# Attention block on one core: the fifth visit's readers exchanged, dense matmuls put ahead of the value products, and the small steps between them rescheduled

## The chip, the core and the metric

The kernel runs on one core of one Trainium2 chip. A core has a matmul engine (PE, with PEld for its weight loads), a vector engine (DVE), an activation engine (ACT), a general engine (POOL) and a queue that issues transfers (SP), each with its own instruction stream[...]. The metric is the device time of one execution in microseconds (us).

## The reference

Input `x` is 4 batches of 512 tokens by 512 features. Everything is float32.

```
x = x + attention(layernorm(x))     # 32 query heads, 8 key/value heads, head size 16, rotary, causal
x = x + (silu(h @ Wg.T) * (h @ Wu.T)) @ Wd.T,   h = layernorm(x)      # inner size 1376
```

The softmax is over the keys of each query, with the query's own largest score taken off first.

## The kernel before

**Dense work.** Projections, the output projection and the feed-forward part are called dense work here. They are cut into steps of four matmuls, each matmul 32 output columns wide while attention runs (L240), so that four lie side by side in the array. Batch b's input is normalised, turned so that features lie on the partitions (`xnT`), and projected to queries, keys and values (`projections`, L327). Batches 0 and 2 are turned by PE (`transposed`, L242). Batches 1 and 3 are turned by DVE and transfers (`flipped`, L252): DVE transposes blocks into `xt`, SP writes them to `flip` in memory with four transfers (L259), and reads each tile of 128 tokens back into `xnT` with one (L261). The last tile's read has to wait for its own four writes.

**Groups.** Attention runs over 32 groups of four heads, eight groups a batch. The loop `slot(b, ...)` (L790) holds batch b's eight groups and fills the gaps between their score matmuls with dense steps of other work. While group g gets its final scores ("less", L557, whose query rows `qa` already hold the largest score), group g+2 gets plain scores (L544), of which DVE finds the largest for each query.

**Visits.** Each group has five visits to the two score tiles `sc`, of two PSUM banks each. In visits 1 to 4 the first tile always holds plain scores of two heads and the second holds less scores of the two other heads. DVE reads the first tile (`greatest`, L586), ACT takes the exponential of the second (L645), POOL zeroes what lies past the diagonal (`causal`, L647). The next visit's matmuls overwrite the same tiles. In visit 5 (`last_visit`, L607) every bank holds both kinds, less scores in its first half and plain ones in its second, so ACT and DVE both want each bank. ACT takes the first tile, then the second; DVE follows it, the first tile, then the second. The framework that records the kernel makes two readers of one bank wait for each other in program order. Then come the largest scores turned and written to memory (`turned_round`, L626), from where SP lays them into a later group's `qa` (`laid_out`, L633), and the value products `av` (`averages`, L664), which read the exponentials after POOL has zeroed them. POOL also makes a fresh `qa` (`masked`, L523, L529) right after visit 5's zeroing; the next visit 1 starts with it.

**Order of the work around the change.** `gap(n)` puts dense steps after visit n+1; in slot 0 (`thin`) the shares are 0.2, 0.225, 0.2875 and 0.2875 of a group's dense work, in the others five shares, the last after the value products. `odd_steps(us)` (L213) puts small steps of DVE behind each visit's `greatest`: first `later` if a value product is unread, then `aside` (statistics, normalisations, turning), then the filled projection banks of `full` (rotary: L303, L307 on DVE, L304, L308 on POOL), then the rest of `later`. `holding` makes `put` keep back some POOL instructions from the end of visit 4 until `release` after visit 5. Normalisation of batches 2 and 3 is a DVE shift (L198) and an ACT scaling (L199), not kept back. Batch 2's input is loaded in `begin2`, which the opening (L766 to L788), where groups 0 and 1 get their plain scores, calls among its dense steps.

Of the kernel before, what the change touches and what calls it, by code (L numbers as in the profile page):

```python
# [14 lines left out]
AF = mybir.ActivationFunctionType  # L15
# [3 lines left out]
B, T, D = 4, 512, 512  # L19
NH, NKV, DH = 32, 8, 16  # L20
FF = 1376
P = 128
NT = T // P
# [26 lines left out]
GROUPS = [(b, m, hf) for b in range(B) for m in range(4) for hf in range(2)]  # L50
# [24 lines left out]
def preln_block_kernel(  # L75
# [13 lines left out]
    nc = tc.nc  # L89
# [18 lines left out]
    for rows, at, base in ((slice(0, P), T - P, 0), (slice(0, 64), T, 64), (slice(64, P), T, 0)):  # L108
# [4 lines left out]
            fill=MASKED,  # L113
# [50 lines left out]
    full = deque()  # L164
# [14 lines left out]
    def load_xr(b, i):  # L179
        t = work.tile([P, D], F32, tag="xr", name="xr", bufs=6)  # L180
        nc.sync.dma_start(out=t, in_=x[b, ts(i, P), :])
        xr[b, i] = t

    def statistics(src):
        st = small.tile([P, 6], F32, tag="st", name="st")
        mv = small.tile([P, 2], F32, tag="mv", name="mv")
        rstd = small.tile([P, 1], F32, tag="rstd", name="rstd")
        nc.vector.bn_stats(st, src)  # L188
        nc.vector.bn_aggr(mv, st)
        nc.vector.tensor_scalar(rstd, mv[:, 1:2], EPS, None, ALU.add)  # L190
        nc.gpsimd.tensor_tensor(rstd, rstd, neghalf, ALU.pow)
        return src, mv, rstd

    def normalised(dst, found, by_act=False):
        src, mv, rstd = found
        if by_act:
            shift = mv[:, 1:2]
            nc.vector.tensor_scalar(shift, mv[:, 0:1], rstd, -1.0, ALU.mult, ALU.mult)  # L198
            nc.scalar.activation(dst, src, AF.Identity, bias=shift, scale=rstd)  # L199
        else:  # L200
            nc.vector.tensor_scalar(dst, src, mv[:, 0:1], rstd, ALU.subtract, ALU.mult)

# [7 lines left out]
        for _ in range(min(n, len(queue))):  # L210
            queue.popleft()[1]()

    def odd_steps(us, banks=True):  # L213

        for n in range(len(soon)):
            left, step = soon.popleft()
            if left > 0:
                soon.append((left - 1, step))
            else:
                aside.appendleft(step)  # L220
        while True:
            queue = (unread and later) or aside or (banks and full and full[0]) or later
            if not queue:
                return
            us -= queue[0][0]
            if us < -0.15:
                return
            do(queue)
            if full and not full[0]:
                full.popleft()  # L230
# [52 lines left out]
        steps = [lambda ps, k=k, h=h: product(ps, k, ts(h, 2 * P)) for h in range(2) for k in range(NK)]  # L283
        return [(0.43, step) for step in portions(steps, finish, 8)]

    held = deque()
    holding = [False]

    def put(step):
        held.append(step) if holding[0] else step()

    def release():
        while held:
            held.popleft()()

    def rotated(ps, dst, engine=nc.gpsimd):

        rot = work.tile([P, T], F32, tag="rot", name="rot", bufs=4)  # L300
# [23 lines left out]
            cost, step = steps[kind]  # L324
            yield cost, lambda step=step, i=int(i): step(i)

    def projections(b, n, early=False):  # L327

        home, xa, found, xn, ready = homes[n], {}, {}, {}, []
        xnT = xnT_of[b]  # L330

        def load(i):
            if early:
                xa[i] = xr[b, i]
            else:
                xa[i] = work.tile([P, D], F32, tag="xa", name="xa", bufs=4)
                nc.sync.dma_start(out=xa[i], in_=x[b, ts(i, P), :])

        def measure(i):
            found[i] = statistics(xa[i])  # L340

        def norm(i):
            xn[i] = work.tile([P, D], F32, tag="xa", name="xa", bufs=4) if early else xa[i]
            normalised(xn[i], found[i], by_act=b > 1)

        def flip(i):
            if b % 2:
                flipped(xn[i], i, 1, xnT)
            ready.append(i)

        def keys():
            def finish(ps):
                kr = work.tile([P, T], F32, tag="rot", name="kr", bufs=4)

                def spread():
                    release()
                    ks = work.tile([P, T], F32, tag="rot", name="ks", bufs=4)
                    nc.vector.stream_shuffle(ks, kr, SWAP)
                    for t, hf, src in ((0, 0, kr), (1, 1, kr), (0, 1, ks), (1, 0, ks)):
                        put(  # L360
                            lambda t=t, hf=hf, src=src: nc.gpsimd.tensor_scalar(
                                home[:, 4 + 2 * t + hf, :], src, halves[hf], (one16, one0)[hf], ALU.mult, ALU.add
                            )
                        )

                last = spread if early else lambda: soon.append((1, (0.75, spread)))
                return [*rotated(ps, kr, nc.vector if early else nc.gpsimd), (0.0, last)]

            return projected(wk_sb, 0, xnT, finish)

        def vals():
            def product(ps, i, k):
                for c in (0, 64) if i == NT - 1 else ():
                    token = P * i + 64 - c
                    product_of(
                        ps[c : c + 64, ts(i, P)], xnT[:, k, token : token + 64], wv_sb[:, k, :], k == 0, k == NK - 1
                    )
                if i < NT - 1:
                    product_of(ps[:, ts(i, P)], xnT[:, k, ts(i, P)], wv_sb[:, k, :], k == 0, k == NK - 1)

            def finish(ps):
                def copy():
                    nc.scalar.copy(
                        values(n)[:, :, :, DH : 2 * DH].rearrange("p i g d -> p (i g) d"),
                        ps.rearrange("p (a d) -> p a d", d=DH),
                    )

                return [(0.0, copy)]

            steps = [lambda ps, i=i, k=k: product(ps, i, k) for i in range(NT) for k in range(NK)]  # L390
            return [(0.45, step) for step in portions(steps, finish, 8)]

        def queries(m):
            engine = nc.vector if early and m == 0 else nc.gpsimd
            return projected(wq_sb, m, xnT, lambda ps: rotated(ps, home[:, m, :], engine))

        def begin():
            for i in range(NT):
                load(i)
            if b > 1:  # L400
                aside.extend(both_steps_apart(measure, norm, flip, 0.75 if b % 2 else 0.0))
            else:
                aside.extend(both_steps(measure, norm, flip, flip_us=0.75 if b % 2 else 0.0))

        def tail(i):
            while i not in ready:
                do(aside)
            if b % 2 == 0:
                transposed(xn[i], i, xnT)

        turned = [(0.0 if b % 2 else 0.45, lambda i=i: tail(i)) for i in range(NT)]
        rest = [*keys(), *queries(0), *vals()]
        for m in range(1, 4):
            rest += queries(m)
        return (0.0, begin), turned, rest

    def attended(b, by_pe=()):

# [188 lines left out]
    def last_visit(h, g):  # L607

        for r in range(4):
            less_score(g, r, 2, pairs[r // 2][:, r % 2, : 2 * P])  # L610
        if h < len(GROUPS):
            for half in (64, 0):
                for r in range(4):
                    plain_half(h, r, 1, pairs[r // 2][:, r % 2, 2 * P :], half)
        for n in (0, 1):
            heads = slice(2 * n, 2 * n + 2)
            exponentials(e2[:, heads, :], pairs[n][:, :, : 2 * P])
            causal(e2, 0, heads)
        holding[0] = False
        masked(g + 3)  # L620
        release()
        if h < len(GROUPS):
            for r in range(4):
                greatest(h, r, 1, pairs[r // 2][:, r % 2, 2 * P :])

    def turned_round(g):  # L626
        if g >= len(GROUPS):
# [90 lines left out]
    for t in low:  # L718
# [2 lines left out]
    nc.sync.dma_start(out=rope_sb, in_=rope)  # L721
    load_columns(wq_sb, wq, 0, P)

    (begin1, turned1, rest1), (begin2, turned2, rest2), (begin3, turned3, rest3) = (
        projections(b, b) for b in range(1, B)
    )
    begin, turned, start = projections(0, 0, early=True)
    begin[1]()
    do(aside, len(aside))
    begin1[1]()  # L730
# [34 lines left out]

    thin[0] = True  # L766
    opening = deque([*start[28:], *turned1, begin2, *rest1[:16]])
    each = sum(cost for cost, _ in opening) / 6
    done = 0.0
    for h in range(2):  # L770
        for n, entries in enumerate((((0, 3),), ((0, 2), (3 * P, 0)), ((0, 1),))):
# [8 lines left out]
            odd_steps((1.5, 1.0, 2.7 - h)[n])  # L780
            if h == 0:
                nc.gpsimd.memset(values(n + 1), 1.0)
            done = fill(opening, each * (3 * h + n + 1), done)
        if h == 0:
            laid_out(0)
            masked(2)
# [3 lines left out]
    def slot(b, steps):  # L790
# [7 lines left out]

        def gap(n):
            nonlocal done, part  # L800
            part += total * ((0.2, 0.225, 0.2875, 0.2875) if thin[0] else (0.19, 0.19, 0.22, 0.22, 0.18))[n] / 8
            done = fill(steps, part, done)

        for g in groups:
            h = g + 2
            laid_out(g + 1)
            for n, visit in enumerate(visits):
# [12 lines left out]
                    causal(e1, 3 * P, exchanged=True)  # L820
                all_greatest(h, visit)
                holding[0] = n == 3
                odd_steps((1.3, 0.95, 0.95, 1.05)[n] if thin[0] else 2.3, n < 3)
                gap(n)
            last_visit(h, g)
            turned_round(h)
            averages(g)
            odd_steps(1.4)
            if not thin[0]:
                gap(4)  # L830
        thin[0] = narrow[0] = False
        emptied(len(full))
        if b == B - 1:
# [90 lines left out]
```

## Time and profile before

| what | value |
|---|---|
| median of 3 runs (lowest to highest) | 893.87 us (893.75 to 894.65) |
| the profiled execution's own time | 893.94 us |
| its span | 892.2 us |
| PE busy | 865.6 us, 97% of the span |
| DVE busy | 469.6 us, 53% |
| POOL busy | 234.5 us, 26% |
| ACT busy | 204.6 us, 23% |
| slot 0, groups 0 to 7 | 51.38 to 179.03 us |
| slots 1 to 3 | 179.03 to about 734 us |
| dense tail on PE alone | to the end |

Times in the trace count from the first instruction. DVE is busy for 6 to 8 tenths of each fortieth of the span up to about 180 us and mostly for 4 to 5 tenths from there to the dense tail, and not at all evenly within a group: a share over the whole run says little about the place where a stage waits.

### The profile page before, as it was taken

Reading aid. Unit: us, or ns where it says so; the run is one execution under the profiler, and the core shown is the slowest. Engines: PE = TensorE matmul, PEld = TensorE weight load, DVE = VectorE, ACT = ScalarE, POOL = GpSimd, SP = SyncE. Lnnn points to the kernel's source line nnn. Section 1 sums busy time; section 2 is a strip of 40 time slices with the busy share of each in tenths; the row PEclk is TensorE's granted clock in tenths of the full one; section 3 lists DMA queues with packets and bytes.
Section 4 is the critical chain, followed back from the end, with each engine's and each line's share of the span. In section 5 each row is a group of like instructions: output and inputs, shape, how many; then the busy total and the mean of one; then the engine's idle time right before and its main releaser. Section 6 shows DMA issues by size and latency. Waiting matters only on the chain.

```text
span 892.2 us, 23910 instructions
## 1 busy us (share of the span) xinstructions
PE 865.6 (97%) x10142; PEld 352.8 (40%) x10142; DVE 469.6 (53%) x1481; ACT 204.6 (23%) x256; POOL 234.5 (26%) x358
## 2 busy tenths in 40 slices
PE   6989999998999999999999999999999999999998
PEld 5644444543333333333333333333333334444443
DVE  7886887777555554485554544575555214121110
ACT  1034443322232222222222222222222220000000
POOL 5555575653312112232112222231221211000000
PEclk9999999999999999999999999999999999999999
DMA  8410141005515110524121110242111203523000
GB/s 247 85 50 5 51 74 29 4 4 121 180 50 176 44 50 14 191 41 117 52 52 44 36 50 14 63 85 84 51 50 50 68 13 80 131 72 82 19 12 35
DMA packets 122762, 59.68 MB, mean 67 GB/s; under 512 B 60480, under 2 KB 114752, under 8 KB 122400
## 3 DMA queue, kind: packets, MB, share of 16 engines
q1 hardware_dynamic: 122368, 52.39, 22.6%
q10 hardware_dynamic: 288, 5.77, 1.7%
q8 instruction: 80, 1.31, 0.6%
q14 instruction: 26, 0.21, 0.1%
HBM read 44.76 MB, written 13.37 MB: 65 GB/s over the span
## 4 chain that ended last, share of the span: by engine, by line
PE 81%; DVE 10%; POOL 2%; DMA 2%; issue 2%; SPq 1%; ACT 1%; POOLq 0%; DVEq 0%; ACTq 0%
PE mm L240 41%; PE mm L237 17%; PE sc L544 12%; PE av L672 6%; DVE junk L590 5%; PE sc L557 4%; POOL e L650 1%; DVE st L188 1%; DVE rot L303 1%; ACT e L645 1%; POOL qa L529 1%; DMA lowest<-turned 1%; SPq L259 0%; PE mm L245 0%; DVE xr L440 0%
## 5 line engine op out<-in xcount | busy, mean ns | idle before, releaser
L590 DVE CUSTOM_DVE_ANT_0 junk<-sc,mask 128x128 f32<-128x128 f32 (+3 forms) x512 | 251.2, 491 | 155.9 <-PE sc L557 93.1
L240 PE MATMUL mm<-xnT,shared 128*32 128x512 f32 (+1 forms) x2704 | 281.9, 545 | 1.0 <-ACT xnT L250 1.0
L645 ACT ACTIVATE e<-sc 128x1024 f32<-128x1024 f32 (+1 forms) x192 | 165.5, 881 | 413.9 <-PE sc L557 334.8
L650 POOL TENSOR_SCALAR_AFFINE_SELECT e<-e 128x512 f32<-128x512 f32 (+2 forms) x192 | 105.6, 560 | 367.5 <-ACT e L645 364.4
L544 PE MATMUL sc<-home,qa 32*64 32x512 f32 (+6 forms) x2048 | 157.8, 422 | 10.9 <-DVE low L590 8.4
L557 PE MATMUL sc<-qa,home 32*64 32x512 f32 (+6 forms) x2048 | 153.1, 428 | 2.7 <-DVE low L590 2.2
L240 PEld LDWEIGHTS mm<-xnT,shared 128*32 128x32 f32 x2704 | 88.0, 109 | 157.5 <-issue 142.1
L544 PEld LDWEIGHTS sc<-home,qa 32*64 32x64 f32 x2048 | 67.4, 131 | 113.4 <-issue 39.6
L237 PE MATMUL mm<-xnT,shared 128*128 128x512 f32 (+2 forms) x256 | 94.7, 528 | 0.0
L240 PE MATMUL mm<-wd_sb,home 128*32 128x512 f32 (+1 forms) x808 | 94.7, 595 | 0.0
L672 PE MATMUL av<-e,home 128*32 128x512 f32 (+3 forms) x1024 | 80.6, 437 | 1.2 <-POOL e L650 1.1
L495 DVE SCALAR_TENSOR_TENSOR g<-g,mm 128x512 f32<-128x512 f32 (+1 forms) x44 | 30.3, 688 | 96.6 <-ACT g L494 96.6
L557 PEld LDWEIGHTS sc<-qa,home 32*64 32x64 f32 x2048 | 58.8, 130 | 31.8 <-issue 14.2
L237 PEld LDWEIGHTS mm<-xnT,shared 128*128 128x128 f32 (+1 forms) x256 | 48.0, 189 | 46.6 <-issue 44.7
L237 PE MATMUL mm<-wd_sb,home 128*128 128x512 f32 (+1 forms) x150 | 65.0, 593 | 0.0
L494 ACT ACTIVATE g<-mm 128x512 f32<-128x512 f32 (+1 forms) x44 | 26.3, 597 | 168.8 <-PE mm L237 109.6
L497 DVE TENSOR_TENSOR home<-mm,g 128x512 f32<-128x512 f32 (+1 forms) x44 | 30.4, 691 | 57.2 <-PE mm L240 34.0
L513 DVE SCALAR_TENSOR_TENSOR xr<-mm,xr 128x512 f32<-128x512 f32 x16 | 11.0, 689 | 76.4 <-PE mm L237 56.2
L672 PEld LDWEIGHTS av<-e,home 128*32 128x32 f32 x1024 | 31.1, 109 | 44.6 <-issue 36.6
L240 PEld LDWEIGHTS mm<-wd_sb,home 128*32 128x32 f32 (+1 forms) x808 | 28.3, 110 | 50.6 <-issue 49.6
L240 PE MATMUL mm<-wo_sb,cx 128*32 128x512 f32 x384 | 45.0, 595 | 0.0
L237 PEld LDWEIGHTS mm<-wd_sb,home 128*128 128x128 f32 (+1 forms) x150 | 28.4, 190 | 36.3 <-issue 36.3
(73 smaller groups left out, 454.0 us busy)
## 6 DMA issues: line engine op xcount, KB each, us to landing
shared<-in_wg SPq DMA_DIRECT2D x40, 256.0 KB
shared<-in_wu SPq DMA_DIRECT2D x40, 256.0 KB
flip<-xt SPq DMA_DIRECT2D x88, 64.0 KB
xnT<-flip SPq DMA_DIRECT2D x18, 256.0 KB
xr<-in_x SPq DMA_DIRECT2D x16, 256.0 KB
out<-xr SPq DMA_DIRECT2D x16, 256.0 KB
xa<-in_x SPq DMA_DIRECT2D x12, 256.0 KB
spill<-wd_sb ACTq DMA_DIRECT2D x1, 2816.0 KB
```

Source lines behind the costliest of these rows:

```text
L237: nc.tensor.matmul(out, lhsT=lhsT, rhs=rhs, start=start, stop=stop)
L240: nc.tensor.matmul(out[c : c + 32], lhsT=lhsT[:, c : c + 32], rhs=rhs, start=start, stop=stop)
L494: nc.scalar.activation(gs[f][:m, :], ps[:m, :], AF.Tanh, scale=0.5)
L495: nc.vector.scalar_tensor_tensor(gs[f][:m, :], gs[f][:m, :], 1.0, ps[:m, :], ALU.add, ALU.mult)
L497: nc.vector.tensor_tensor(homes[n][:m, f, :], ps[:m, :], gs[f][:m, :], ALU.mult)
L513: nc.vector.scalar_tensor_tensor(xr[b, i], py[i], 0.5, xr[b, i], ALU.mult, ALU.add)
L544: nc.tensor.matmul(dst[at : at + 64, :n], lhsT=qa[g][rows_of(r), q : q + 64], rhs=keys_of(g)[rows_of(r), :n], start=True, stop=True,)
L557: nc.tensor.matmul(dst[at : at + 64, first_q:], lhsT=keys_of(g)[rows_of(r), k : k + 64], rhs=qa[g][rows_of(r), P * j + first_q :], start=True,
L590: nc.vector.tensor_tensor_reduce(out=junk[:, :n], in0=src, in1=mask[:, T - n : T] if i else mask[:, T:], scale=-1.0, scalar=BIG, op0=ALU.a ...
L645: nc.scalar.activation(dst, src, AF.Exp, scale=1.0 / math.sqrt(DH))
L650: nc.gpsimd.affine_select(out=e[rows, heads, c : c + P], in_=e[rows, heads, c : c + P], compare_op=ALU.is_ge, fill=0.0, base=base, pattern ...
L672: nc.tensor.matmul(av[32 * r : 32 * r + 32, P * j :], lhsT=v[:, j, 4 * (m // 2) + r, DH * (1 - hf) : DH * (3 - hf)], rhs=e[:, r, c : c + n ...
```

## The change

Six edits, all in the order in which instructions are recorded; no arithmetic is added or removed.

1. In visit 5, DVE reads the second tile first while ACT takes the first, then they exchange. ACT's exponential of the second tile now waits for DVE's two reads there.
2. Dense steps stand between visit 5 and the value products in every slot. In slots 1 to 3 the fifth share moves there from behind the value products. In slot 0 a fifth share, 0.077, is new, and visits 2 to 4 give it up.
3. `odd_steps` may put rotary steps of a filled bank ahead of `aside` after visit 1.
4. ACT's scaling of batches 2 and 3 goes through `put`, so it is kept back from visit 4 to the end of visit 5 when its step falls there; `flip` releases it.
5. Batch 2's input is loaded when batch 1's last tile has been turned, not in `begin2`.
6. The opening's dense steps are spread 0.3, 0.38 and 0.32 over its three visits instead of evenly.

Edits 3 and 5 also shift small steps to other visits. On DVE in slot 0 the order behind each visit becomes the following (the groups of the loop; st = statistics, sh = shift, xt = turning, us = reading of `av`, cx = turning of the context, ks = key shuffle, rot and cos = rotary):

```
group: before visit 1's reads | after visit 1 | after 2 | after 3 | after 4     (before -> after)
0: st sh | st sh rot cos | st | ks sh rot cos | sh      ->  st sh | rot cos | st | ks sh rot cos | st
1: us | - | rot | cos | -                               ->  us sh sh | - | rot | cos | -
3: us | st sh | st rot cos | xt sh | st rot cos         ->  us | rot cos | st | st | sh rot cos
4: us | ks | xt sh | sh xt rot cos | xt                 ->  us | rot cos | ks | st | xt sh
5: cx | us | rot | cos | -                              ->  cx | us | st | xt sh | sh xt rot cos
6: us | rot cos | rot | cos | cx                        ->  us | rot cos | xt | rot | cx cos
```

On ACT the two scalings of batch 2's last tiles now stand together, behind group 0's fifth visit and ahead of the values' copy (L383) and of group 1's first exponential. On SP batch 2's four loads stand ahead of the first write of `lowest`. Batch 3's last tile is turned in group 6 (after visit 2) instead of group 4 (after visit 4). On PE the second half of batch 3's keys, which reads that tile's part of `xnT`, is in group 6 between visits 3 and 4.

```diff
@@ statistics / normalised
-            nc.scalar.activation(dst, src, AF.Identity, bias=shift, scale=rstd)
+            put(lambda: nc.scalar.activation(dst, src, AF.Identity, bias=shift, scale=rstd))
@@ odd_steps
-    def odd_steps(us, banks=True):
+    def odd_steps(us, banks=1):
...
-            queue = (unread and later) or aside or (banks and full and full[0]) or later
+            bank = full and full[0]
+            queue = (unread and later) or (banks == 2 and bank) or aside or (banks and bank) or later
@@ projections
-    def projections(b, n, early=False):
+    def projections(b, n, early=False, then=None):
...
         def flip(i):
+            if b > 1:
+                release()
             if b % 2:
                 flipped(xn[i], i, 1, xnT)
             ready.append(i)
+            if i == NT - 1 and then:
+                then()
...
-        def begin():
+        def load_all():
             for i in range(NT):
                 load(i)
+
+        def begin():
+            if not xa:
+                load_all()
@@ last_visit
         for n in (0, 1):
             heads = slice(2 * n, 2 * n + 2)
             exponentials(e2[:, heads, :], pairs[n][:, :, : 2 * P])
             causal(e2, 0, heads)
+            if h < len(GROUPS):
+                for r in (2 - 2 * n, 3 - 2 * n):
+                    greatest(h, r, 1, pairs[r // 2][:, r % 2, 2 * P :])
         holding[0] = False
         masked(g + 3)
         release()
-        if h < len(GROUPS):
-            for r in range(4):
-                greatest(h, r, 1, pairs[r // 2][:, r % 2, 2 * P :])
@@ the opening
-    (begin1, turned1, rest1), (begin2, turned2, rest2), (begin3, turned3, rest3) = (
-        projections(b, b) for b in range(1, B)
-    )
-    begin, turned, start = projections(0, 0, early=True)
+    begin3, turned3, rest3, _ = projections(3, 3)
+    begin2, turned2, rest2, load2 = projections(2, 2)
+    begin1, turned1, rest1, _ = projections(1, 1, then=load2)
+    begin, turned, start, _ = projections(0, 0, early=True)
...
-    each = sum(cost for cost, _ in opening) / 6
+    each = sum(cost for cost, _ in opening) / 2
...
-            done = fill(opening, each * (3 * h + n + 1), done)
+            done = fill(opening, each * (h + (0.3, 0.68, 1.0)[n]), done)
@@ slot
-            part += total * ((0.2, 0.225, 0.2875, 0.2875) if thin[0] else (0.19, 0.19, 0.22, 0.22, 0.18))[n] / 8
+            part += total * ((0.2, 0.2, 0.2615, 0.2615, 0.077) if thin[0] else (0.19, 0.19, 0.22, 0.22, 0.18))[n] / 8
...
-                odd_steps((1.3, 0.95, 0.95, 1.05)[n] if thin[0] else 2.3, n < 3)
+                odd_steps((1.3, 0.95, 0.95, 1.05)[n] if thin[0] else 2.3, (2, 1, 1, 0)[n])
                 gap(n)
             last_visit(h, g)
             turned_round(h)
+            gap(4)
             averages(g)
             odd_steps(1.4)
-            if not thin[0]:
-                gap(4)
```

## The prediction, made before the run

> **What bounds the kernel now.** I read the page's busy shares and its chain first, then the timeline of single groups, then windows at the places where groups differ.
>
> ```profile
> PE 865.6 (97%) x10142; PEld 352.8 (40%) x10142; DVE 469.6 (53%) x1481; ACT 204.6 (23%) x256; POOL 234.5 (26%) x358
> ...
> PE 81%; DVE 10%; POOL 2%; DMA 2%; issue 2%; SPq 1%; ACT 1%; POOLq 0%; DVEq 0%; ACTq 0%
> ```
>
> PE sets the end, and DVE is the only other engine with weight on the chain. Group starts (first plain scores in the timeline) tell where. In slots 1 to 3 most groups take 23.29 us or less, and PE has no wait but its own changes between dense and score matmuls. In slot 0 the starts are 51.38, 70.83, 86.01, 101.11, 117.49, 133.70, 148.78, 163.92 and 179.03, so groups last 19.45, 15.18, 15.10, 16.38, 16.21, 15.08, 15.14 and 15.11 us. There DVE paces PE: the interval between visits 3 and 4 is 3.0 us both with 12 dense matmuls (group 2) and with 16 (group 5), and the dense phase with its wait is 2.06 us in each. Moving dense work out of these visits saves nothing. Groups 0, 3 and 4 are longer because DVE's small steps overfill the cover that a visit's scores give them (0.95 to 1.05 us, about 1.15 to 1.25 with latency).
>
> An ordinary end of a group in slot 0, from the timeline:
>
> ```profile
> 160.49 0.69 PE L557 MATMUL sc<-qa,home 32*64 32x256 f32 x16
> 161.43 2.44 PE L672 MATMUL av<-e,home 128*32 128x512 f32 x32
> 161.63 1.08 ACT L645 ACTIVATE e<-sc 128x512 f32<-128x512 f32 x2 [1.89 <-PE sc L544]
> 162.26 0.42 DVE L590 CUSTOM_DVE_ANT_0 junk<-sc,mask 128x256 f32<-128x256 f32 x1 [1.20 <-ACT e L645]
> 162.35 0.83 POOL L650 TENSOR_SCALAR_AFFINE_SELECT e<-e 128x256 f32<-128x256 f32 x2 [0.62 <-ACT e L645]
> 163.17 0.69 POOL L529 TENSOR_SCALAR qa<-home,rope_sb 128x512 f32<-128x512 f32 x1
> 163.92 0.64 PE L544 MATMUL sc<-home,qa 32*64 32x512 f32 x2
> ```
>
> DVE waits 0.63 us for ACT's first exponential. The next visit 1 starts right after `qa` (163.86) and then pauses 0.33 us more for DVE's last bank.
>
> Where slot 0 starts, DVE waited for batch 2's input, PE stood still (49.56 to 51.38), and its clock was then granted at half:
>
> ```profile
> 48.11 0.69 DVE L188 BATCH_NORM_STATS2 st<-xa 128x6 f32<-128x512 f32 x1 [2.05 <-DMA xa<-in_x]
> ```
> ```profile
> 50.00:52.00 2.00, 0.62 (x4) 0.22 (x4) 1.79 (x8) 0.00 (x0) 1.92 (x2) 1.00 0.02 7
> 52.00:54.00 2.00, 2.00 (x15) 0.32 (x12) 1.52 (x7) 0.34 (x1) 0.96 (x2) 0.60 0.05 8
> 54.00:56.00 2.00, 2.00 (x42) 1.62 (x40) 1.59 (x5) 1.46 (x2) 0.14 (x1) 0.55 0.04 9
> ```
>
> (The last three numbers are granted clock, DMA share, GB/s.) Visit 1's scores took 2.89 us there instead of 1.04.
>
> **The opening and group 0.** The loads ahead of `lowest` end the 2.05 us wait. PE then comes to visit 1 at 49.5, when its dense work ends; DVE clears the second tile at 52.28 - 2.05 = 50.2; scores end near 51.15 instead of 54.27, at full clock. On SP the four loads cost 1.87 us of issue and 3.6 us of data (DMA share 0.96 at 47 to 48) ahead of `lowest` and the five `qa` transfers: group 0's rows land near 48.3 instead of 46.5 and are used at 49.5, so 0, and up to 1.0 if the queue is slower. From there POOL sets group 0's end: key shuffle (8 us after the scores), two L361 (1.52), rotary (1.28 + 1.27), visit 4's zeroing (1.92), the newly placed rstd (0.55), visit 5's zeroing (0.84), `qa` (0.69): 67.2 against 70.83. **-3.6**; bounds -2.4 (loads late, clock falls anyway) and -4.
>
> **Ordinary groups of slot 0.** DVE is ready 0.65 us earlier, so visit 1's pause of 0.33 goes. But ACT's second exponential now follows DVE's two reads (161.6 + 0.95), then come its 0.55, zeroing 0.41, `qa` 0.69: 164.25, 0.4 later than before; the new dense step (0.43) and `av` (2.4) end at the same time. **+0.05** a group, four or five of them: +0.2. This chain now has no slack, and a small step behind visit 4 over 1.1 us passes through whole (before, ACT's 0.6 covered it too).
>
> **Groups 1, 3, 4, 5.** Group 1: the two shifts wait for `us`, which waits for `av`. From the end of `av`: us and reciprocal 0.92, shifts 0.4, scalings from 1.14 to 2.76 (814 ns each), values' copy to 3.35 (585), exponential to 4.37 (1.02). Visit 2's less scores need that tile at about 2.9: +1.45, **+1.4** with visit 1's pause gone. Queued behind the wait on ACT: that copy and all exponentials. Group 3: 1.42 us behind visit 4 overfill by 0.3, and the double load behind visit 2 is gone: 16.38 to 15.45. Group 4: no overfill, 16.21 to 15.15. Together **-2.0**. Group 5: shift, turning and rotary (2.03) behind visit 4: **+0.9**.
>
> **Group 6.** Batch 3's last tile is turned behind visit 2's reads, and keys that read it come one dense step after visit 3's scores. The trace has every link:
>
> ```profile
> 33.03 0.71 DVE L255 STREAM_TRANSPOSE xt<-xa 128x512 f32<-128x512 f32 x1
> ...
> 33.76 1.93 SPq L259 DMA_DIRECT2D flip<-xt  x4
> 35.81 1.81 SPq L261 DMA_DIRECT2D wd_sb<-flip  x2
> ```
> ```profile
> 129.80 2.77 DMA xnT<-flip
> ```
>
> The last write is issued 1.45 after the transposition, the last tile's read at 37.24, 2.05 after that, and a read takes 2.7: 6.2 us. From group 6's start: visit 2's scores end at 3.7, DVE's reads at 5.15, transposition 5.8, data at 12.0. PE comes to these keys at 6.7 (visit 3 from 5.33, scores 0.95, one step 0.43). After the data two steps and the change (1.02) bring visit 4 at 13.0 instead of 8.34: +4.7, and nothing later hides it; behind it queue visit 4's scores, so DVE and ACT too. Before, the same read was issued at 134.59 and first used after 150. For the clock after this 5.3 us stand there are two answers. Here it fell after 1.82 us of stillness. The Trainium skill ("TensorE: Matmul & The Clock Gate", Part 1) lets it fall after an idle window of some 3.4 us that runs free, and rise after a busy one; by that page 5.3 us need not hold a whole window, and the price is between 0 and 1.7. By the row it falls surely: 3.4 us at half are 1.7, less what DVE's pace hides, 1.5. I take the row: **+6.2**; with the page's other end +4.7. The page would also have let the start of slot 0 keep its clock; the row of 52 to 54 says otherwise.
>
> **Slots 1 to 3.** The same dense work stands on the other side of `av`. Three waits lose their place: in group 8 `av` waited 0.7 for zeroing behind an rstd, and visit 1 0.33; group 9's visit 1 to 2 lost 0.9 to DVE's additions, whose matmuls now end 2.4 us earlier; group 16's `av` waited 0.7. Sum -2.7. The change from `av` to scores took 0.24 in slot 0, from dense 0.21: +0.03 for 22 groups, +0.6. **-2.1**; bounds -3.3 and -0.8. The longer wait of ACT's second exponential lies under 1.7 us or more of dense work and costs nothing; without that cover it is 0.4 a group.
>
> **The sum**: -3.6 + 0.2 + 1.4 - 2.0 + 0.9 + 6.2 - 2.1 = +1.0. Against the profiled execution's own 893.94 (0.07 over the median, so the same) that is **895.0 us**. A change under 0.2% (1.8 us) is about what a measurement of this kernel can't tell from none: 892.1 to 895.7.
>
> **Rivals.** (a) The transfer of group 6 is quicker: 4 us instead of 6.2, clock kept: 895.0 - 2.2 - 1.5 = 891.3. For it: these transfers come alone, where those of 33 and 130 us had others beside them. Against: the 2.05 is the wait for one's own writes and the 2.7 a single read. (b) Slower: the clock falls in group 0's end or group 1 too. In group 0 PE would wait some 2.1 of 3.4 us between value products for POOL, in group 1 1.9 us for ACT; the stillness that made it fall at 52 was 1.8 of 3.4. Each fall costs up to 1.7: 898.4. It decides where half of such a window is still. (c) The exchange and the move do nothing that counts, gains and losses of slot 0 being as small as its ordinary groups': 893.9.
>
> **Chances.** The likeliest case 0.48, its own range 893.4 to 897.0, about a third of it over 895.7; (a) 0.22; (b) 0.20; (c) 0.10. Slower 0.17 + 0.20 + 0.01 = 0.38; same 0.31 + 0.08 = 0.39; faster 0.23. The range reaches to (a)'s and (b)'s values and their spread of about 1 us: 890.5 to 898.6.
>
> **What would show it.** Group 0 starts near 49.5 at clock 1.0; POOL, not PE, ends it. Group 1's visit 2 waits for ACT. In group 6 a wait of PE near 5 us for `xnT`, and a clock under 1 after it. Ordinary groups stay at 15.1. Slots 1 to 3: no wait of `av` for POOL. The prediction falls if group 6 lasts under 18 us, or if ordinary groups leave 15.1 by more than 0.3.

## The result, and the profile after

The changed kernel takes 898.3 us (median of four runs, 897.34 to 899.73) against 894.13 before: a ratio of 1.0049, 95% interval 1.0035 to 1.0062. It is slower by half a per cent. The profiled execution took 899.73 us with a span of 897.9, so it is the slowest of the four, 1.4 us over the median; why is told below with e4.

The page's busy shares and its chain, after:

```profile
PE 866.2 (96%) x10142; PEld 340.5 (38%) x10142; DVE 471.9 (53%) x1481; ACT 207.8 (23%) x256; POOL 234.3 (26%) x358
...
PE 81%; DVE 11%; issue 3%; POOL 2%; DMA 2%; ACT 1%; SPq 1%; POOLq 0%; DVEq 0%; ACTq 0%
```

Busy times of PE, DVE, ACT and POOL are those of before within 3.2 us. Nearly all the difference is waiting, and the page says nothing of where. Group starts do. The table has the length of each group in slot 0, from its first plain scores to those of the next (timeline), in us; the last two columns are kernels of the experiments.

| group | before | predicted difference | after | difference | turned early (e1) | e1 without slot 0's exchange (e5) |
|---|---|---|---|---|---|---|
| start of slot 0 | 51.38 | | 51.11 | -0.27 | 49.64 | 50.38 |
| 0 | 19.45 | with the start -3.6 | 18.25 | -1.20 | 18.34 | 18.39 |
| 1 | 15.18 | +1.4 | 16.86 | +1.68 | 15.70 | 15.18 |
| 2 | 15.10 | +0.05 | 15.71 | +0.61 | 15.70 | 15.09 |
| 3 | 16.38 | with group 4 -2.0 | 15.91 | -0.47 | 17.45 | 16.38 |
| 4 | 16.21 | | 15.61 | -0.60 | 16.60 | 16.21 |
| 5 | 15.08 | +0.9 | 16.20 | +1.12 | 15.61 | 15.23 |
| 6 | 15.14 | +6.2 | 24.05 | +8.91 | 15.61 | 15.10 |
| 7 | 15.11 | +0.05 | 15.49 | +0.38 | 15.61 | 15.10 |
| slots 1 to 3, to the end | 713.17 | -2.1 | 708.74 | -4.43 | 708.75 | 708.86 |

The differences add to +5.7, that of the two spans.

**Where slot 0 starts.** The timeline of DVE has no wait at batch 2's first tile any more (before: 2.05 us), and windows of the same place show PE busy throughout at whole clock (before: 0.60 and 0.55):

```profile
47.60 0.69 DVE L200 BATCH_NORM_STATS2 st<-xa 128x6 f32<-128x512 f32 x1
```
```profile
50.00:52.00 2.00, 2.00 (x16) 1.07 (x20) 1.75 (x10) 0.00 (x0) 1.92 (x2) 1.00 0.00 0
52.00:54.00 2.00, 2.00 (x58) 1.19 (x54) 1.90 (x8) 0.85 (x2) 0.59 (x2) 1.00 0.10 16
```

**An ordinary end of a group**, from the timeline without its weight loads (group 2; the prediction showed group 6 of before):

```profile
97.86 0.69 PE L566 MATMUL sc<-qa,home 32*64 32x256 f32 x16 [0.56 <-DVE low L599]
98.25 0.63 PE L553 MATMUL sc<-home,qa 32*64 32x256 f32 x16
98.81 0.64 PE L253 MATMUL mm<-xnT,shared 128*32 128x256 f32 x8
99.00 0.60 ACT L655 ACTIVATE e<-sc 128x512 f32<-128x512 f32 x1 [1.89 <-PE sc L553]
99.11 0.42 DVE L599 CUSTOM_DVE_ANT_0 junk<-sc,mask 128x256 f32<-128x256 f32 x1 [1.30 <-PE sc L553]
...
100.13 0.60 ACT L655 ACTIVATE e<-sc 128x512 f32<-128x512 f32 x1 [0.52 <-DVE low L599]
...
100.80 0.41 POOL L660 TENSOR_SCALAR_AFFINE_SELECT e<-e 128x256 f32<-128x256 f32 x1 [0.65 <-ACT e L655]
...
101.19 0.69 POOL L538 TENSOR_SCALAR qa<-home,rope_sb 128x512 f32<-128x512 f32 x1
...
101.93 0.65 PE L553 MATMUL sc<-home,qa 32*64 32x512 f32 x2
```

The exchange does what it says: DVE starts 0.11 after ACT's first exponential instead of 0.63. But ACT's second exponential now waits 0.52 for DVE, POOL waits for ACT, `qa` waits for POOL, and PE starts the next group with `qa`: 4.07 us after visit 5's first scores (97.86), where it was 3.43 (160.49 to 163.92 in the prediction's rows).

**Group 1**, from the timeline: visit 2's less scores wait a whole microsecond for the exponential, which stands behind the two scalings and the copy.

```profile
70.44 1.52 ACT L211 ACTIVATE xa<-xa,mv,rstd 128x512 f32<-128x512 f32 x2 [3.23 <-DVE mv L210]
...
71.87 0.56 ACT L388 COPY home<-mm 128x512 f32<-128x512 f32 x1
...
72.33 1.02 ACT L655 ACTIVATE e<-sc 128x1024 f32<-128x1024 f32 x1
73.41 0.14 PEld L566 LDWEIGHTS sc<-qa,home 32*64 32x64 f32 x2 [1.00 <-ACT e L655]
```

**Group 6**, from the chain that ended last, in this stretch (start, length, what), with everything from the last turned tile to the keys that read it:

```profile
155.22 0.64 DVE xt L268
...
155.88 0.32 SPq L272
...
156.24 1.92 SPq L272
...
158.20 0.49 SPq L272
...
158.74 1.98 DMA flip<-xt
...
160.85 2.93 DMA xnT<-flip
...
163.92 1.94 PE mm L253 x16
```

The timeline has the same stop as one row, a 7.05 us wait of PE for `xnT` that ends at 163.92. In the windows the clock (third number from the end) falls with it:

```profile
158.00:160.00 2.00, 0.00 (x0) 0.00 (x0) 0.88 (x4) 0.00 (x0) 1.04 (x1) 1.00 0.52 80
160.00:162.00 2.00, 0.00 (x0) 0.00 (x0) 0.00 (x0) 0.00 (x0) 0.22 (x1) 0.81 0.60 156
162.00:164.00 2.00, 0.08 (x4) 0.11 (x8) 0.00 (x0) 0.00 (x0) 0.00 (x0) 0.50 0.42 126
164.00:166.00 2.00, 2.00 (x24) 0.80 (x32) 0.00 (x0) 0.00 (x0) 0.00 (x0) 0.50 0.00 0
166.00:168.00 2.00, 2.00 (x40) 1.13 (x37) 0.32 (x1) 0.20 (x1) 0.00 (x0) 0.50 0.00 0
168.00:170.00 2.00, 2.00 (x48) 1.11 (x48) 1.90 (x9) 0.83 (x1) 1.09 (x2) 0.98 0.00 0
```

### The profile page after: what moved, and what is told of

Its sections match the earlier page's. It is cut to its first block, busy times and chain, and to the rows that moved or that the text cites. A ratio compares the mean times of both kernels' runs of the same rounds, so it can differ in the third digit from the quotient of the medians.

```text
span 897.9 us, 23914 instructions
## 1 busy us (share of the span) xinstructions
PE 866.2 (96%) x10142; PEld 340.5 (38%) x10142; DVE 471.9 (53%) x1481; ACT 207.8 (23%) x256; POOL 234.3 (26%) x358
## 4 chain that ended last, share of the span: by engine, by line
PE 81%; DVE 11%; issue 3%; POOL 2%; DMA 2%; ACT 1%; SPq 1%; POOLq 0%; DVEq 0%; ACTq 0%
PE mm L253 42%; PE mm L250 17%; PE sc L553 12%; DVE junk L599 6%; PE av L682 6%; PE sc L566 4%; POOL e L660 1%; ACT e L655 1%; DVE st L200 1%; POOL qa L538 1%; DVE rot L304 1%; SPq L272 1%; DVE home L308 1%; DMA xr<-in_x 1%; DMA flip<-xt 0%
## 5 line engine op out<-in xcount | busy, mean ns | idle before, releaser
L655 ACT ACTIVATE e<-sc 128x1024 f32<-128x1024 f32 (+1 forms) x192 | 168.8, 883 | 430.4 <-PE sc L566 334.0
L253 PEld LDWEIGHTS mm<-xnT,shared 128*32 128x32 f32 x2704 | 79.5, 110 | 174.2 <-issue 157.7
L682 PEld LDWEIGHTS av<-e,home 128*32 128x32 f32 x1024 | 33.0, 110 | 50.1 <-issue 43.9
L696 DVE STREAM_TRANSPOSE us<-av 128x512 f32<-128x512 f32 x32 | 22.9, 716 | 44.8 <-PE av L682 44.8
L253 PEld LDWEIGHTS mm<-wd_sb,home 128*32 128x32 f32 (+1 forms) x808 | 23.9, 109 | 55.1 <-issue 53.9
```

The lines of the kernel that those rows point to most:

```text
L253: nc.tensor.matmul(out[c : c + 32], lhsT=lhsT[:, c : c + 32], rhs=rhs, start=start, stop=stop)
L655: nc.scalar.activation(dst, src, AF.Exp, scale=1.0 / math.sqrt(DH))
L682: nc.tensor.matmul(av[32 * r : 32 * r + 32, P * j :], lhsT=v[:, j, 4 * (m // 2) + r, DH * (1 - hf) : DH * (3 - hf)], rhs=e[:, r, c : c + n ...
L696: nc.vector.transpose(t, av)
```

## The experiments

Three questions were open: whether the late turning alone makes the loss; what each of the other edits is worth by itself; and of what group 6's 8.9 us consist. The kernel before was timed again beside them: 893.97 us with e1, e2, e4 and e5, 893.93 with e3, e6, e8 and e9, and 894.09 with e10.

### The changed kernel with the turning early again (e1)

```
-                odd_steps((1.3, 0.95, 0.95, 1.05)[n] if thin[0] else 2.3, (2, 1, 1, 0)[n])
+                odd_steps((1.3, 0.95, 0.95, 1.05)[n] if thin[0] else 2.3, (1, 1, 1, 0)[n])
```

> The changed kernel without edit 3: rotary steps keep their place behind the statistics, normalisations and turning after visit 1, so batch 3's last tile is turned in group 5 (after visit 2) and batch 2's two late scalings leave group 1. Theory (the late turning makes the loss): group 6 falls from 24.05 to about 15.6 us and group 1 from 16.86 to about 15.5; no half clock near 160; 898.3 - 8.4 - 1.3 = 888.6 us. Rival (the turning is only one of several late steps; another wait takes its place in group 4, 5 or 7): group 6 back under 16, but a neighbour longer by 3 us or more, 892 or above. Rival (the exchange in slot 0 is what costs): under 2 us gained, 896.5 or above.

Measured: 890.95 us, 0.9969 of the kernel before (0.9958 to 0.9981), 7.35 below the changed kernel. The whole loss and more hangs on this one argument. The table shows how: group 6 gives back 8.44 and group 1 1.16, as expected, and group 5 another 0.59. The 2.35 us that are missing from the expected 888.6 are in groups 3 and 4, which are 1.54 and 0.99 longer than in the changed kernel: there edit 3 had relieved visits that DVE's small steps overfill. So edit 3 is good for about 2.5 us in groups 3 and 4 and costs about 10.2 in groups 1, 5 and 6.

### Dense steps ahead of the value products, in slots 1 to 3 alone (e2)

```
             turned_round(h)
+            if not thin[0]:
+                gap(4)
             averages(g)
             odd_steps(1.4)
-            if not thin[0]:
-                gap(4)
```

> The kernel before with one part of edit 2: in slots 1 to 3 the fifth share of dense steps stands ahead of the value products; visit 5, slot 0 and the loads are as before. Theory (the place of the dense work alone makes the gain of slots 1 to 3): the stretch from slot 1's start to the end falls from 713.2 to about 708.7 us as in the changed kernel, and the time to 894.1 - 4.4 = 889.7. The prediction's own number for this part, -2.1, would give 892.0. Rival (the gain needs the exchange of visit 5, by which DVE's banks come free earlier): less than 1 us, 893.1 or above.

Measured: 889.26 us, 0.9949 (0.9937 to 0.9962), 4.7 below the kernel before. Slots 1 to 3 last 708.46 us, a little less than in the changed kernel: this part needs no exchange. The first three rows below are PE's timeline at the end of an unhurried group in the kernel before, the second three the same group's end in e2:

```profile
269.68 2.44 PE L672 MATMUL av<-e,home 128*32 128x512 f32 x32
271.86 1.98 PE L240 MATMUL mm<-xnT,shared 128*32 128x512 f32 x16
273.77 0.64 PE L544 MATMUL sc<-home,qa 32*64 32x512 f32 x2
```
```profile
267.72 1.92 PE L240 MATMUL mm<-xnT,shared 128*32 128x512 f32 x16
269.46 2.34 PE L672 MATMUL av<-e,home 128*32 128x512 f32 x32
271.73 0.65 PE L544 MATMUL sc<-home,qa 32*64 32x512 f32 x2
```

From start to start the two kinds of work take 4.09 us in the one order and 4.01 in the other. So an unhurried group is 0.08 shorter; the rest is in the groups with a wait: 8 (24.49 to 23.57), 9 (25.39 to 24.41), 16 (24.14 to 23.21) and 26 (22.65 to 22.35).

### The early load alone (e4)

```
             ready.append(i)
+            if i == NT - 1 and then:
+                then()
...
+        def load_all():
             for i in range(NT):
                 load(i)
+
+        def begin():
+            if not xa:
+                load_all()
...
+    begin1, turned1, rest1, _ = projections(1, 1, then=load2)
```

> The kernel before with edit 5 alone: batch 2's input is loaded when batch 1's last tile has been turned. Theory (the wait for that input stood alone on the path and its stillness took the clock): slot 0 starts near 49.5 us instead of 51.38, group 0 lasts 17.5 to 18.3 instead of 19.45, the clock stays whole: 894.1 - 3.2 = 890.9. Rival (loads on SP ahead of the largest scores put off group 0's rows): slot 0 starts near 51, gain under 1 us, 893.1 or above. A later first rise of the clock in the opening, 1.5 us as seen in the changed kernel's trace, can hide it in a single run; over several it should average out.

Measured: 891.51 us, 0.9975 (0.9965 to 0.9985), 2.46 below the kernel before. Slot 0 starts at 50.31, group 0 lasts 18.39, the clock stays whole, and all later groups are those of before within 0.15 us. It gained less than the 3.2 expected, for a reason that the traces of all kernels share. PE's clock starts at half (in the changed kernel the matmuls of the first projection start 0.427 us apart before the rise and 0.216 after it) and rises once in the opening, at another time in each execution; slot 0's start follows it. From the records of the granted clock and the timeline (the last three rows without the early load):

| kernel | clock first whole, us | slot 0 starts, us |
|---|---|---|
| e1 | 11.64 | 49.64 |
| e6 | 11.97 | 49.47 |
| e10 | 13.00 | 50.20 |
| e8 | 13.33 | 50.21 |
| e5 | 13.47 | 50.38 |
| e4 | 13.58 | 50.31 |
| e9 | 14.23 | 50.62 |
| after | 14.49 | 51.11 |
| before | 11.42 | 51.38 |
| e2 | 11.57 | 51.48 |
| e3 | 14.56 | 52.97 |

From e6 to e9 the rise is 2.26 later and slot 0 starts 1.15 later, as half a clock would have it (from e1 to the changed kernel 2.85 and 1.47). The same delay shows without the early load, from e2 to e3, but there little of it is left at the end of group 0: before and e2 lost the clock at slot 0's start and ended group 0 at 70.83 and 70.86; in e3 PE stood still there just as long (1.87 us, before 1.82) and the clock stayed whole, and group 0 ended at 71.56, with the exchange in it. It fits the profile of the changed kernel: its rise was late, and its time is the highest of the four.

### Both of these together (e8), and the same with one more step (e9)

e8 is e2's and e4's edits on the kernel before. e9 adds edit 3's priority for group 4 alone:

```
-                odd_steps((1.3, 0.95, 0.95, 1.05)[n] if thin[0] else 2.3, n < 3)
+                odd_steps((1.3, 0.95, 0.95, 1.05)[n] if thin[0] else 2.3, 2 if n == 0 and g ==4 else n < 3)
```

> The kernel before with two parts of the change alone: edit 5 (batch 2's input loaded when batch 1's last tile has been turned) and, in slots 1 to 3, the fifth share of dense steps ahead of the value products. No exchange anywhere. Theory (these two are all that the change gains, and they add): 893.97 - 2.46 - 4.71 = 886.8 us; slots 1 to 3 last 708.5 us. Rival (in slots 1 to 3 the exchange gives something of its own): the kernel with the exchange there was 886.9, so this one would be above 887.5.

> The kernel with the early load and the dense steps ahead of the value products in slots 1 to 3, and edit 3's priority of rotary steps behind visit 1 of group 4 alone, where batch 3's last tile is then turned in group 5 after visit 1. Theory (edit 3 costs only where it pushes the last turning past its cover): group 4 falls from 16.21 to about 15.2 because nothing overfills visit 4, group 5 rises by 0.3 at most: 886.8 - 0.7 = 886.1 us. Rival (the turned tiles are late even so): a wait for xnT in group 6, 888 or above.

Measured: e8 887.19 us, 0.9924 (0.9912 to 0.9937); e9 886.72, 0.9917 (0.9904 to 0.9931). The two gains add, within 0.4 us. In e9 group 4 falls from 16.22 to 15.13 and group 5 rises from 15.08 to 15.55, with no wait for `xnT` in group 6: the traces show 0.6 us gained, the times can't tell it from none. Both kernels beat the kernel before and the changed one.

### The exchange: slots 1 to 3 alone (e5), and everywhere without dense cover (e3)

e5 is e1 with the old visit 5, the old shares and no dense step ahead of the value products in slot 0:

```
             causal(e2, 0, heads)
-            if h < len(GROUPS):
+            if h < len(GROUPS) and not thin[0]:
                 for r in (2 - 2 * n, 3 - 2 * n):
                     greatest(h, r, 1, pairs[r // 2][:, r % 2, 2 * P :])
         holding[0] = False
         masked(g + 3)
         release()
+        if h < len(GROUPS) and thin[0]:
+            for r in range(4):
+                greatest(h, r, 1, pairs[r // 2][:, r % 2, 2 * P :])
...
             turned_round(h)
-            gap(4)
+            if not thin[0]:
+                gap(4)
             averages(g)
```

> The changed kernel with edit 3 undone and, in slot 0 alone, the old visit 5 (DVE behind ACT in both tiles), the old four shares and no dense step ahead of the value products. Theory (in slot 0 the exchange costs 0.6 us in each ordinary group and gives nothing back; in slots 1 to 3 it does no harm): slot 0 from 49.5 to about 174.5 us, slots 1 to 3 as in the changed kernel, 708.7 after it: 885 to 887 us, 2 us or more below the kernel without edit 3 alone. Rival (the exchange gains in slot 0 too once the late turning is gone): not below the kernel without edit 3, 888.6 or above.

Measured: 886.9 us, 0.9924 (0.9912 to 0.9937), 4.05 below e1. In slot 0 the exchange, with the fifth share that goes with it, costs 4 us and gives nothing back: every group of e1 from group 1 on is 0.4 to 1.1 longer than that of e5. In slots 1 to 3 it does nothing: e8, without it there, is the same within the measurement.

e3 is the kernel before with edit 1 alone:

```
             causal(e2, 0, heads)
+            if h < len(GROUPS):
+                for r in (2 - 2 * n, 3 - 2 * n):
+                    greatest(h, r, 1, pairs[r // 2][:, r % 2, 2 * P :])
         holding[0] = False
         masked(g + 3)
         release()
-        if h < len(GROUPS):
-            for r in range(4):
-                greatest(h, r, 1, pairs[r // 2][:, r % 2, 2 * P :])
```

> The kernel before with edit 1 alone: the exchange in visit 5, with the value products right behind it in every slot. Theory (the second exponential, now behind two of DVE's reads, sets the end of the group wherever no dense work stands between): slot 0's groups about 15.6 instead of 15.1 (8 times 0.5 = 4), and in slots 1 to 3 the value products wait for the later zeroing, by 0.4 (the prediction's number) to 0.75 us in 23 groups, 9 to 17: 907 to 915 us. Rival (the value products have slack there): slots 1 to 3 unchanged at 713.2, 898 us.

Measured: 912.13 us, a ratio of 1.02 (1.0184 to 1.0215). Slots 1 to 3 last 727.14 instead of 713.17, 0.6 us a group. The timeline at the end of an unhurried group of theirs:

```profile
277.48 0.60 ACT L645 ACTIVATE e<-sc 128x512 f32<-128x512 f32 x1 [0.43 <-DVE low L590]
...
278.14 0.41 POOL L650 TENSOR_SCALAR_AFFINE_SELECT e<-e 128x256 f32<-128x256 f32 x1 [0.56 <-ACT e L645]
...
278.60 0.11 PEld L672 LDWEIGHTS av<-e,home 128*32 128x32 f32 x2 [0.48 <-POOL e L650]
...
278.62 0.62 PE L240 MATMUL mm<-xnT,shared 128*32 128x512 f32 x2
...
278.84 0.39 PE L672 MATMUL av<-e,home 128*32 128x256 f32 x2
```

The last value products wait until POOL's zeroing ends at 278.55; in the kernel before they had room. So the dense work ahead of `av` is what makes the exchange harmless in slots 1 to 3, and not the other way round. In slot 0 e3's ordinary groups (5 to 7) last 15.61 us, as those of e1 do: the exchange alone makes the loss there, and the fifth share adds nothing to it.

### Group 6 taken apart: the writes on two queues (e6), and PE kept at work (e10)

e6, on the changed kernel: of the four writes of the last turned tile two go through ACT's queue.

```
         for r in range(4):
             rows = t[32 * r : 32 * r + 32, :]
-            nc.sync.dma_start(out=turned[i, r], in_=rows.rearrange("d (c s) -> d c s", s=32))
+            queue = nc.scalar if n and i == last and r % 2 and narrow[0] and thin[0] else nc.sync
+            queue.dma_start(out=turned[i, r], in_=rows.rearrange("d (c s) -> d c s", s=32))
```

> The changed kernel, but two of the four writes of batch 3's last turned tile go through ACT's queue instead of SP's. It measures the disputed cost in group 6: there the four writes took 3.36 us to issue on SP, one of them 1.92, against 1.93 for all four at 33.76 us before. Theory (SP's issue is on the path of group 6): the data arrive 1.0 to 2.4 us earlier, group 6 lasts 21.6 to 23.1 us instead of 24.05, the whole 896 to 897.3. Rival (the time is set by the writes and the read themselves, not by their issue): group 6 within 0.5 us of 24.05.

Measured: 897.21 us, 1.0037 (1.0023 to 1.005); group 6 lasts 22.68, 1.37 less. The timeline of SP and ACT (a q marks a queue's issue):

```profile
154.09 0.85 SPq L273 DMA_DIRECT2D flip<-xt  x2
155.04 2.81 SPq L275 DMA_DIRECT2D xnT<-flip  x2
```
```profile
154.09 0.93 ACTq L273 DMA_DIRECT2D flip<-xt  x2
```

All four writes are issued after 0.93 us instead of 3.36, and PE's wait for `xnT` falls from 7.05 to 5.26: 1.8 of the 2.4 us come through, the rest goes mostly into the last write's landing, 2.84 us on the chain instead of 1.98. The group gains less than the wait, because here PE worked 5.2 us at half clock behind the data (160.34 to 165.57), in the changed kernel 4.2 (163.92 to 168.09).

e10, on the changed kernel: 14 extra dense steps, whose products are overwritten, stand where PE waits.

```
-    def projected(w, m, xnT, finish):
+    def projected(w, m, xnT, finish, filler=0):
         def product(ps, k, at):
+            if k == 0 and at.start:
+                for _ in range(filler):
+                    product_of(ps[:, at], w[:, k, ts(m, P)], xnT[:, k, ts(0, 2 * P)], True, True)
...
-            return projected(wk_sb, 0, xnT, finish)
+            return projected(wk_sb, 0, xnT, finish, filler=14 if b == 3 else 0)
```

> The changed kernel with 14 extra dense steps (56 matmuls whose products are overwritten) at the place in group 6 where PE waits for xnT, some 6.0 of its 7.07 us, so that PE isn't still there while the wait itself stays. It measures the disputed price of the clock. Theory (the row: the stillness takes the clock, and the half clock costs 1.7 us that nothing hides): no half clock near 160, group 6 lasts 22.3 us instead of 24.05, the whole 896.6. Rival (the other end: the price hides under the pace of DVE): group 6 within 0.4 us of 24.05, the whole 898.3. Rival (the extra matmuls run past the data's arrival): group 6 above 24.5.

Measured: 897.09 us, 1.0038 (1.0024 to 1.0052). PE's timeline has the filler and what is left of the wait; the window after it has a whole clock:

```profile
155.25 6.68 PE L253 MATMUL mm<-xnT,shared 128*32 128x256 f32 x120
162.56 1.07 PE L253 MATMUL mm<-xnT,shared 128*32 128x256 f32 x16 [0.64 <-DMA xnT<-flip]
```
```profile
162.00:164.00 2.00, 1.44 (x32) 0.82 (x40) 0.00 (x0) 0.00 (x0) 0.00 (x0) 1.00 0.04 9
```

Group 6 lasts 21.87, 2.18 less with 6 us more work in it. Some 0.4 of that is the transfer, whose data came 7.7 us after the first write's issue (154.90 to 162.56) instead of 8.0 (155.88 to 163.92); about 1.8 is the clock.

## Why the prediction was right and wrong

The time lies in the range (890.5 to 898.6) and 3.3 us above the predicted value, outside the likeliest case's own 893.4 to 897.0. It is close to rival (b)'s 898.4, yet (b)'s mechanism did not happen: the clock stayed whole in group 0 and group 1. The mechanisms of the likeliest case are all there. Four of its terms were mis-sized, three to one side and one to the other. That the time is in the range is luck in this: it lies 0.3 us inside an upper end that had been drawn for (b). The path from one kernel to the other, by the runs:

| step | us |
|---|---|
| before (mean of the batches) | 894.0 |
| early load (e4) | -2.5 |
| dense steps first in slots 1 to 3 (e2) | -4.7 |
| both together (e8); with the exchange in slots 1 to 3, the opening's shares and held scalings (e5) | 887.2; 886.9 |
| exchange and fifth share in slot 0 (e1) | +4.05, 890.95 |
| rotary steps first behind visit 1 (after) | +7.35, 898.3 |

**The opening and group 0** (predicted -3.6). Right in kind: no wait of DVE, whole clock, start at 49.5 with an early rise of the clock. The size is that of a lucky execution: with an early rise group 0 ends at 67.7 to 68.0 (e6, e1) against the predicted 67.2 and 70.83 before, and the average gain is 2.5 (e4). Group 0 itself took 18.2 to 18.4 in every kernel with the early load, not 17.7. POOL ends it, as predicted: in the changed kernel it works almost without a pause from 65.93 to the end of `qa` at 69.30.

**Ordinary groups of slot 0** (predicted +0.05 each). This step failed, by the sign that the prediction itself had set (ordinary groups off 15.1 by more than 0.3): it is +0.4 to +0.6, and through groups 1 to 7 it makes the 4.05 us of e1 over e5. Two terms of the working were off. The chain to `qa` takes 4.07 instead of 3.82, because DVE's first read starts only when the second tile's scores end (1.25 after the first instead of 1.11) and each handover adds a little. And visit 1's pause of 0.33 does not go: 0.22 of it stays although DVE has been done with its banks since 101.05. Between the first plain and the first less scores the trace has semaphore instructions of PE's queue there, by which it waits for several others (two, at 101.94 and 102.05; in the kernel before three, from 101.11 on); where it has none, as at 104.79, the less scores start 0.01 behind. So most of the pause had been no wait for DVE. The prediction's warning that this chain has no slack was right: in e1 a group whose visit 4 is overfilled pays twice (group 3, 17.45 against 16.38).

**Groups 1, 3, 4 and 5** (+1.4, -2.0, +0.9; measured +1.68, -1.07, +1.12). With the ordinary loss of about 0.5 taken off each they are +1.2, -2.1 and +0.6: the working was right. Group 1 is shown by e1, where the scalings are elsewhere and the group is 1.16 shorter. For groups 3 and 4, e9 shows it for group 4 alone (1.09).

**Group 6** (predicted +6.2, measured +8.9). The mechanism was right at each link, the sizes added up short. PE waited 7.05 us, not 5.3: DVE's reads and the transposition were 0.4 later, and the four writes took 3.36 to issue instead of the 1.93 of the row that was used, since one of them took 1.92 by itself. e6 shows that the issue counts: 2.4 us less of it took 1.8 off PE's wait. The write's own 1.98 and the read's 2.93 are near the 2.05 and 2.7 of the rows. Rival (a), a quicker transfer, is refuted.

**The clock.** The half clock, from 161.26 to 168.09 and in its first part spent waiting, cost about 1.8 us by e10. The row had been priced at 1.5, which is 1.7 less what DVE's pace would hide; PE worked 4.17 us at half, worth 2.1, so about as much was hidden as the prediction took, and the time at half was longer. This wait would not have decided between row and page: 7 us hold a whole idle window, and the Trainium skill ("TensorE: Matmul & The Clock Gate", Part 1), too, lets the clock fall then. They differ at the start of slot 0, and there neither holds as it was put. e2 repeats the row: the clock fell at 52.53, after a stretch in which PE was still for little more than half the time. But in e3 PE was still at the same place for 1.87 us and the clock stayed whole. What counts is how much of one stretch of the clock's grid is still (last section), and e3's stillness lay across the border of two, which were busy 0.70 and 0.75. By the same measure (b) did not happen: the emptiest stretch in group 0 was busy 0.63, with PE still for 1.27 us at the longest, not 2.1.

**Slots 1 to 3** (predicted -2.1, measured -4.43, and -4.7 alone). The waits were sized right: 2.7 predicted, and groups 8, 9, 16 and 26 with 17 give -2.9. What failed is the change of order itself, put at +0.03 a group and 0.6 in all. The price of going from value products to scores, 0.24, had been read in slot 0, where the next scores wait for `qa`; in slots 1 to 3 the new order is 0.08 shorter a group, 1.5 gained in the 19 groups without a wait instead of 0.6 lost.

The forecast of about no change was a small difference of large terms: by the runs 7.2 us are gained by two edits and 11.4 lost by the others. Terms too low by some 1 us (the opening, on average), 2.3 (the ordinary loss, in groups 1 to 5 and 7) and 2.7 (group 6), and one too high by 2.3 (slots 1 to 3), decided. Rival (c), that gains and losses are small, is refuted for the same reason.

## What to carry to other kernels

An instruction's wait is worth what lies between it and the next thing that needs it: the same exchange cost nothing with 1.9 us of dense work behind it, 0.5 us a group where the next scores waited for `qa`, and 0.6 where value products followed at once. When small steps are given a new priority, follow the last of those that start a transfer to its first reader: gains of a microsecond in two groups were paid for with nine in another. A price read in a stage that waits for something is not the price of the operation in a stage that doesn't.

## What the runs showed of the hardware

- The changes of PE's granted clock come on a grid: in the records of before, after and e4 they lie 3.41, 6.83, 40.96, 146.77, 730.45, 836.26 and 877.23 us apart, which are 1, 2, 12, 43, 214, 245 and 257 times 3.413.
- The clock fell to half after a stretch of that grid in which PE was busy 0.24 and 0.38 of the time (ends of e10 and e3), 0.45 (e2) and 0.465 (before); it stayed whole after 0.475 (end of e5), 0.50 (end of e2), 0.55 (twice, e1), 0.62 (e10) and 0.63 (after). So the limit lay a little under half busy, as far as the trace's modelled ends of matmuls tell. The length of a stillness alone does not decide: 1.82 us took the clock in before, 1.87 us did not in e3.
- At half the clock stayed at half after stretches that were busy 0.53 (e6), 0.73 (after, opening) and 0.86 (e9, opening), and rose after 0.90 (before, e1, e2, e6) and after full ones.
- The clock's first rise came between 11.4 and 14.6 us after the first instruction, with the same instructions on PE up to there; this moves the start of slot 0 by up to about 1.5 us.
- One of four equal writes in a row can take 1.7 to 2.7 us to issue where the others take 0.3 to 0.8 (in the kernel before at 16.88 and 125.21, after at 17.88 and 156.24). What it waits for the traces do not show, and no run here looked for it.
